# Which engine makes some of layer 3's state sums: 24 additions from VectorE to GpSimd

## The chip, the cores and the metric

The kernel runs on one core of a Trainium2 chip. The core has five engines that work side by side, each through its own queue in order: TensorE (PE in the profile, with its weight loads as PEld), VectorE (DVE), ScalarE (ACT), GpSimd (POOL) and SyncE (SP), which here issues the DMAs. The metric is the device time of one execution in microseconds (us). Before the change it was 6535.2, 6563.37 and 6560.74 us in three runs; the median is 6560.74 us.

## The reference

Four layers are applied to an image `x` of 2 x 128 x 64 x 64: a Mamba block in four directions (layer 0), an attention to a context image (layer 1), a self-attention (layer 2), and a small Mamba block over tokens with a group norm (layer 3). Only layer 3 is touched. Each of the 8192 pixels is a sequence of 8 tokens with 16 channels, so the recurrence has only 8 steps in time, but runs for all pixels at once:

```python
seq = x.transpose(0, 2, 3, 1).reshape(B * H * W, TOKEN_NUM, D_MODEL)   # 8 tokens of 16
dt = jax.nn.softplus(dt @ dt_proj_w.T + dt_proj_b)
dA = jnp.exp(dt[..., None] * A)
dBx = dt[..., None] * Bm[:, :, None, :] * xs[..., None]
def step(h, inp):
    dA_t, dBx_t, C_t = inp
    h = dA_t * h + dBx_t
    return (h, jnp.einsum('nds,ns->nd', h, C_t))
_, ys = jax.lax.scan(step, h0, (dA, dBx, Cm))     # over the 8 tokens
y = (ys + xs * D) * jax.nn.silu(z)
return y @ out_proj_w.T
...
return x + xp        # xp: SiLU of the group norm of the result
```

All is float32. The state `h` has 32 x 16 numbers per pixel.

## The kernel before

Layer 3 cuts the 2 x 4096 pixels into 16 chunks of T = 512 pixels (`ci` = 0 to 15). A chunk has four steps (`k` = 0 to 3), and a step handles two neighbouring tokens (`o` = 0, 1; the first token of step 0 needs no decay, the second of step 3 no sum). For one token the state is a tile of 128 partitions x 4 groups x 512 pixels, and VectorE and GpSimd handle it in two halves of 2 x 512 = 1024 numbers per partition. Each half of each token goes through these operations, which the program abbreviates by a letter:

- `D` (method `db_`, line 1390, VectorE): the term dBx; the B rows, loaded by DMA into the tile D, are multiplied by a PSUM tile `rx` that TensorE made.
- ScalarE (`da_`, line 1397) writes dA = exp(..) into a tile A. One A tile holds both tokens of a step, and there are three of them. It is issued one step ahead.
- `m` (method `mul`, line 1407, GpSimd): A = A * h, where h is the D tile of the token before.
- `v` or `g` (method `add`, line 1412): the sum D = D + A, which is the new state h. `v` means VectorE, `g` means GpSimd. Both operands lie in SBUF.
- `C` (method `hc_`, line 1430, VectorE): A = A * q, where q is a PSUM tile that TensorE (line 1424) spreads from C; it overwrites A, so it comes after the sum has read A. One `C` takes one group of both tokens of a step, and it runs one step later. TensorE then adds the products up into y (line 1440), which releases A.

The two digits behind `m`, `v` and `g` are token and half. The order is written out by hand, with four groups of operations for each step:

```python
PLAN = (
    ("m10 m11 C D", "C D time", "C v10 D", "g11 D C"),
    ("m00 m01 C D v00", "C v01 D m10 m11", "v10 D", "g11 D"),
    ("m00 m01 C D v00", "C v01 m10 m11", "C v10 D", "g11 C"),
    ("m00 m01 C D", "C v00 D g01 m10 m11", "C D", "D C"),
)
```

The program issues these in this order, and each engine takes its own share of them in order. So GpSimd's queue in step 1 and in step 2 is m00 m01 m10 m11 g11, in step 3 m00 m01 g01 m10 m11, in step 0 m10 m11, two more products that `time` stands for (`dt_add`, line 1341, and `dtx_`, line 1344), and g11: 20 operations per chunk. VectorE has 8 sums, 14 `C`, 14 `D` and six small operations in a chunk (lines 1324, 1376, 1445, 1455). The state's dependence runs m00, v00, m10, v10, and then m00 of the next step; the other half runs m01, v01, m11, g11.

GpSimd issues no DMA in layer 3. SyncE's queue loads D and the decays' source dtr for two steps ahead; there are six D tiles.

Of the kernel before, what the change touches and what calls it, by code (L numbers as in the profile page):

```python
# [14 lines left out]
B, C, H, W = 2, 128, 64, 64  # L15
# [41 lines left out]
def conv_seq_kernel(ctx: ExitStack, tc: tile.TileContext, a: dict, out: bass.AP):  # L57
# [40 lines left out]
    with ExitStack() as c0:  # L98
# [397 lines left out]
        with tc.manual_schedule():  # L496
# [114 lines left out]
            for k, c in enumerate(chunks):  # L611
# [3 lines left out]
                def at(u):  # L615
                    return (c, u) if 0 <= u < 16 else ((old, u + 16) if u < 0 else (new, u - 16))
# [3 lines left out]
                A, V, M, G = {}, {}, {}, {}  # L620
# [191 lines left out]
    with ExitStack() as c1:  # L812
# [377 lines left out]
        with tc.manual_schedule():  # L1190
# [22 lines left out]
            for slot in range((len(groups) + 2) * UPG):  # L1213
                u = slot % UPG
                G = at(slot)[0]
# [5 lines left out]
                G, d = at(slot - 1)  # L1221
                if G is not None:
                    G.larger(d)
                G = at(slot - UPG)[0]
# [7 lines left out]
                G, d = at(slot - UPG - 5)  # L1232
                if G is not None and d % 2 == 0:
                    G.prob(d // 2)
                G, d = at(slot - UPG - 6)
                if G is not None and d % 2 == 0:
                    G.expo(d // 2)
                G, d = at(slot - UPG - 8)
                if G is not None:
                    G.value(d)  # L1240
                G, d = at(slot - UPG - 7)
                if G is not None and d % 2 == 0 and d:
                    G.total(d // 2)
                G, d = at(slot - 2 * UPG)
# [13 lines left out]
    with ExitStack() as c3:  # L1258
# [252 lines left out]
        V, G = nc.vector, nc.gpsimd  # L1511
# [9 lines left out]
        def prepare():  # L1521

            nonlocal made
            if made < len(cs):
                c, k, u = cs[made]
                c.pc_(k, u)
                made += 1
# [3 lines left out]

        PLAN = (
            ("m10 m11 C D", "C D time", "C v10 D", "g11 D C"),
            ("m00 m01 C D v00", "C v01 D m10 m11", "v10 D", "g11 D"),
            ("m00 m01 C D v00", "C v01 m10 m11", "C v10 D", "g11 C"),
            ("m00 m01 C D", "C v00 D g01 m10 m11", "C D", "D C"),
        )

# [3 lines left out]
        with tc.manual_schedule():  # L1542
            mm(y, lhsT=ident, rhs=x[:, 0, 0:T], start=True, stop=True)
            c, c1 = chunks[:2]
            c.xs, c.e, c.cb, c.rows, c.ddt = xs0, e0, cb0, rows0, ddt0
            c.spread(0)
            for o in range(2):
                c.load(0, o)
            for o in range(2):
                c.rx_(0, o)  # L1550
            c1.xs = xs1
            c1.dt_(0)
            norms = [Norm(b) for b in range(B)]
            for s in range(-1, len(steps) + 3):
                (pc_, pk), (cc, ck), (nc_, nk) = at(s - 1), at(s), at(s + 1)
                (n2, n2k) = at(s + 2)
                ci, k = divmod(s, 4)
                fut = chunks[ci + 1] if s >= 0 and ci + 1 < len(chunks) else None
                fut2 = chunks[ci + 2] if ci + 2 < len(chunks) else None
                old = chunks[ci - 1] if ci > 0 else None  # L1560
                nrm = norms[0] if ci in (NCH, NCH + 1) else None

                first, extra = {}, {}

                def more(key, *what, at=extra):
                    at.setdefault(key, []).extend(what)

                if fut is not None:  # L1570
                    more((0, 0), fut.b_, at=first)
                    more((0, 1), fut.c_, at=first)
                    more((0, 2), fut.cb_)
                    more((0, 3), fut.put_b, fut.put)
                if old is not None:
                    more((1, 0), lambda: old.yg_(1))
                    more((2, 1), old.xr_, at=first)
                    more((2, 3), old.bn_)
                if cc is not None:
                    more((1, 0), lambda: cc.cbx_(0), at=first)  # L1580
                    more((1, 0), lambda: cc.ecb_(0))
                    more((1, 3), lambda: cc.y0_(0), at=first)
                    more((1, 3), lambda: cc.sz_(0), at=first)
                    more((2, 0), lambda: cc.sz_(1), at=first)
                    more((3, 0), lambda: cc.cbx_(1), at=first)
                    more((3, 0), lambda: cc.yg_(0), lambda: cc.ecb_(1))
                    more((3, 3), lambda: cc.y0_(1), at=first)
                if fut2 is not None and s >= 0:
                    more((1, 1), lambda: fut2.xs_(0), at=first)
                    more((1, 2), lambda: fut2.xs_(1), at=first)  # L1590
                    more((2, 3), lambda: fut2.dt_(0), at=first)
                if fut2 is not None:
                    more((3, 2), lambda: fut2.dt_(1), fut2.e_exp, fut2.e_ln, at=first)
                if 0 <= ci < B:
                    sl = slice(1024 * k, 1024 * k + 1024)
                    more((k, 3), lambda: nc.sync.dma_start(kept[ci][:, sl], x[:, ci, sl]))
                if n2 is not None:
                    more((k, 0), lambda: n2.spread(n2k), lambda: n2.load(n2k, 0))
                    more((k, 1), lambda: n2.load(n2k, 1))
                    more((k, 3), lambda: n2.rx_(n2k, 0), lambda: n2.rx_(n2k, 1))  # L1600
                if ci == NCH:
                    more((3, 2), nrm.first)
                    more((3, 3), nrm.second, nrm.third)
                if ci == NCH + 1:
                    more((0, 1), nrm.fourth)
                    more((1, 2), *[lambda j=j: nrm.silu(j) for j in range(4)])
                    more((1, 2), lambda: nrm.load(0))
                    for j in range(8):
                        at_ = (2 + j // 4, j % 4)
                        if j < 7:  # L1610
                            more(at_, lambda j=j: nrm.load(j + 1))
                        more(at_, lambda j=j: nrm.store(j, (G, V)[j % 2]))

                nd = 0
                for g in range(4):
                    ops = PLAN[k][g].split()
                    if pc_ is None:
                        ops = [o for o in ops if o != "C"]
                    if nc_ is None:
                        ops = [o for o in ops if o != "D"]  # L1620
                    if cc is None:
                        ops = [o for o in ops if o[0] not in "mvg"]
                    if "C" in ops:
                        prepare()


                    if pc_ is not None and pk and g:
                        pc_.y_(pk, g - 1)
                    (older, ok) = at(s - 2)
                    if g == 0 and older is not None and ok:  # L1630
                        older.y_(ok, 3)
                    for f_ in first.get((k, g), []):
                        f_()
                    if g == 0 and nc_ is not None:
                        nc_.da_(nk)
                    for o in ops:
                        if o == "C":
                            c_, k_, u_ = cs[used]
                            c_.hc_(k_, u_)
                            used += 1  # L1640
                        elif o == "D":
                            nc_.db_(nk, nd // 2, nd % 2)
                            nd += 1
                        elif o == "time":
                            if fut is not None:
                                fut.dt_add()
                                fut.dtx_()
                        elif o[0] == "m":
                            cc.mul(ck, int(o[1]), int(o[2]))
                        else:  # L1650
                            cc.add(ck, int(o[1]), int(o[2]), V if o[0] == "v" else G)
                    for f_ in extra.get((k, g), []):
                        f_()
                if s < 0:
                    prepare()
            n1 = norms[1]
            n1.load_all()
            n1.first()
            n1.second()
            n1.third()  # L1660
            n1.fourth()
            for j in range(8):
                if j % 2 == 0:
                    n1.silu(j // 2)
                n1.store(j, V)
# [109 lines left out]
```

## Time and profile before

| What | Value |
|---|---|
| times of three runs, us | 6535.2, 6563.37, 6560.74 |
| the profiled execution's own time (span), us | 6564.3 |
| VectorE busy over the span | 5628.5 us, 86% |
| GpSimd busy over the span | 5420.7 us, 83% |
| layer 3: GpSimd's first and last product (line 1407) start at | 5602.1 us, 6524.6 us |
| sums (line 1412) on VectorE | 128, from 1210 to 3378 ns, median 2461 ns |
| sums (line 1412) on GpSimd | 64, from 2341 to 3358 ns, median 3218 ns |
| products (line 1407) on GpSimd | 224, from 2339 to 3383 ns, median 2361 ns |
| layer 3, 5602 to 6524 us: VectorE, GpSimd, ScalarE, TensorE busy | 856.6, 789.1, 450.1, 808.7 of 922 us |

Layer 3 is the last seventh of the span. All steps are regular but for the first chunk, the end, and chunks 8 and 9, where the group norm and the stores of the first image are woven in. From the start of one chunk on GpSimd to that of the next, the quick ones take 55.64 to 55.77 us (chunks 1, 2, 5, 7, 8, 11, 12 and 13), chunks 4 and 6 take 56.83 us, and chunk 9, with the stores, 71.35 us. A "busy" time of an instruction goes from its start to its end, whatever it does in between.

### The profile page before, as it was taken

Reading aid. Unit: us, or ns where it says so; the run is one execution under the profiler, and the core shown is the slowest. Engines: PE = TensorE matmul, PEld = TensorE weight load, DVE = VectorE, ACT = ScalarE, POOL = GpSimd, SP = SyncE. Lnnn points to the kernel's source line nnn. Section 1 sums busy time; section 2 is a strip of 40 time slices with the busy share of each in tenths; the row PEclk is TensorE's granted clock in tenths of the full one; section 3 lists DMA queues with packets and bytes.
Section 4 is the critical chain, followed back from the end, with each engine's and each line's share of the span. In section 5 each row is a group of like instructions: output and inputs, shape, how many; then the busy total and the mean of one; then the engine's idle time right before and its main releaser. Section 6 shows DMA issues by size and latency. Waiting matters only on the chain. (4 is left out here: it accounts for less than half of the span.)

```text
span 6564.3 us, 66618 instructions
## 1 busy us (share of the span) xinstructions
PE 5817.9 (89%) x20014; PEld 2781.5 (42%) x20014; DVE 5628.5 (86%) x4540; ACT 4487.8 (68%) x7771; POOL 5420.7 (83%) x2543
## 2 busy tenths in 40 slices
PE   8888888888888888888888999999999999898888
PEld 2222222222222222222226888888888788222221
DVE  7999999999999999999997766666666766899997
ACT  7887778877788777887766665555556565555453
POOL 6999999999999999999995666655666566788886
PEclk7888777877788777887779999999999999889897
DMA  6566656566666666556650000000000000877775
GB/s 181 145 156 161 161 142 146 146 150 148 152 155 151 153 152 152 146 146 152 151 137 19 2 4 3 1 1 1 1 1 1 2 6 7 205 173 179 181 180 121
DMA packets 400476, 700.36 MB, mean 107 GB/s; under 512 B 74089, under 2 KB 76658, under 8 KB 399730
## 3 DMA queue, kind: packets, MB, share of 16 engines
q1 hardware_dynamic: 399232, 694.33, 43.3%
q8 instruction: 157, 2.57, 0.2%
q14 instruction: 205, 1.68, 0.1%
q10 hardware_dynamic: 882, 1.78, 0.1%
HBM read 584.53 MB, written 111.28 MB: 106 GB/s over the span
## 5 line engine op out<-in xcount | busy, mean ns | idle before, releaser
L383 POOL TENSOR_TENSOR dbu<-dus,bs 128x1024 f32<-128x1024 f32 x1024 | 2448.1, 2440 | 116.9 <-DVE h L427 98.8
L427 DVE TENSOR_TENSOR_SCAN h<-da,hst,dbu 128x1024 f32<-128x1024 f32 x896 | 2090.9, 2340 | 86.1 <-ACT dbu L411 80.7
L396 ACT ACTIVATE da<-dts,aneg 128x512 f32<-128x512 f32 (+1 forms) x2048 | 1410.1, 689 | 357.1 <-DVE h L427 318.9
L1004 POOL TENSOR_TENSOR sum<-sum,sc 128x1024 f32<-128x1024 f32 x378 | 898.1, 2376 | 504.1 <-ACT sc L999 500.4
L966 ACT COPY sc<-s 128x512 f32<-128x512 f32 x1024 | 596.9, 585 | 767.8 <-PE s L961 639.2
L961 PE MATMUL s<-q,k 128*128 128x256 f32 x4096 | 1053.8, 380 | 9.7 <-ACT lo L919 5.5
L1016 PE MATMUL av<-sc,v 128*128 128x256 f32 x4096 | 1051.2, 380 | 9.1 <-ACT sc L999 9.1
L450 PE MATMUL y<-hc,cst 128*32 128x512 f32 x4096 | 880.4, 753 | 200.2 <-DVE hc L439 186.6
L973 DVE TENSOR_TENSOR mx<-mx,s 128x512 f32<-128x512 f32 x896 | 609.3, 680 | 452.5 <-ACT sc L966 449.2
L439 DVE TENSOR_TENSOR hc<-h,pc 128x1024 f32<-128x1024 f32 x704 | 841.9, 1196 | 9.5 <-PE y L450 7.4
L961 PEld LDWEIGHTS s<-q,k 128*128 128x128 f32 x4096 | 777.0, 191 | 126.9 <-issue 8.8
L1016 PEld LDWEIGHTS av<-sc,v 128*128 128x128 f32 x4096 | 768.0, 190 | 112.9 <-ACT sc L999 14.1
L437 POOL TENSOR_TENSOR hc<-h,cs 128x1024 f32<-128x1024 f32 x320 | 770.0, 2406 | 1.2 <-issue 1.2
L416 PE MATMUL pc<-xd,sel 16*128 16x512 f32 x1024 | 707.0, 780 | 0.2
L1407 POOL TENSOR_TENSOR A<-A,D 128x1024 f32<-128x1024 f32 x224 | 526.9, 2370 | 138.8 <-DVE D L1412 102.1
L996 DVE TENSOR_TENSOR sc<-sc,pm 128x1024 f32<-128x1024 f32 x512 | 620.5, 1212 | 0.9 <-PE pm L992 0.9
L999 ACT ACTIVATE sc<-sc 128x1024 f32<-128x1024 f32 x512 | 541.8, 1058 | 41.2 <-DVE sc L996 41.0
L450 PEld LDWEIGHTS y<-hc,cst 128*32 128x32 f32 x4096 | 125.9, 120 | 858.3 <-DVE hc L439 427.6
L340 PE MATMUL misc<-xd,w_dt 9*128 9x512 f32 x504 | 364.6, 810 | 128.1 <-ACT x L479 68.5
L411 ACT ACTIVATE dbu<-hst,dbu,df 128x1 f32<-128x1 f32 x896 | 337.6, 377 | 65.3 <-POOL dbu L383 42.7
L1424 PE MATMUL q<-xs,room 32*128 32x512 f32 x840 | 291.1, 706 | 63.1 <-DVE A L1430 62.1
L416 PEld LDWEIGHTS pc<-xd,sel 16*128 16x128 f32 x1024 | 181.6, 218 | 350.2 <-issue 296.8
(315 smaller groups left out, 7792.9 us busy)
## 6 DMA issues: line engine op xcount, KB each, us to landing
dts<-ddt SPq DMA_DIRECT2D x512, 256.0 KB, 5.4
dus<-ddu SPq DMA_DIRECT2D x512, 256.0 KB, 5.1
D<-rows SPq DMA_DIRECT2D x448, 256.0 KB, 6.0
bs<-rows SPq DMA_DIRECT2D x1024, 64.0 KB, 4.9
cs<-rows SPq DMA_DIRECT2D x1024, 64.0 KB, 3.2
ddt<-dt SPq DMA_DIRECT2D x128, 256.0 KB, 2.0
ddu<-dtu SPq DMA_DIRECT2D x128, 256.0 KB, 4.0
dtr<-ddt SPq DMA_DIRECT2D x448, 64.0 KB, 2.0
```

What stands on the lines that cost most here:

```text
L383: nc.gpsimd.tensor_mul(t, self.dus[q], _bc(self.bs[g], 1, [P, 2, T]))
L396: act(t[:, i, sl], self.dts[q][:, i, sl], AF.Exp, scale=an[:, g, 2 * q + i : 2 * q + i + 1])
L416: mm(t, lhsT=sel[32:48, 4 * g : 4 * g + 4, :].rearrange("p n d -> p (n d)"), rhs=self.xd[32:48, :], start=True, stop=True)
L427: nc.vector.tensor_tensor_scan(ho, ai, bi, init, ALU.mult, ALU.add)
L437: nc.gpsimd.tensor_mul(t, self.h[u], _bc(self.cs[gq(u)[0]], 1, [P, 2, T]))
L439: nc.vector.tensor_mul(t, self.h[u], _bc(self.pc[u // 2], 1, [P, 2, T]))
L450: mm(self.y[q // 2][r : r + 32, :], lhsT=sum4, rhs=self.hc[u][:, i, :], start=False, stop=(u % 8 >= 6), skip_group_check=True)
L961: mm(p[:, o, :], lhsT=j.k[m // 8][:, m % 8 * P : m % 8 * P + P], rhs=self.q, start=True, stop=True)
L973: nc.vector.tensor_max(self.mx, self.s[0][:, 0:2, :] if u == 1 else self.mx, self.p[u])
L996: nc.vector.tensor_sub(s, s, _bc(self.pm[:, :], 1, [P, 4, NQ]))
L1004: self.adds.tensor_add(self.sum, self.s[0] if w == 1 else self.sum, self.s[w])
L1016: mm(self.av, lhsT=self.job.v[m // 8][:, m % 8, :], rhs=self.s[u // 2][:, m % 4, :], start=(m == 0), stop=(m == 31))
```

## The change

The third of VectorE's three sums in step 2, v10, becomes g10 in all 16 chunks. The one in step 1 becomes h10, a new letter, which means VectorE in chunks of odd `ci` and GpSimd in those of even `ci`. The place in the plan stays. So 16 + 8 = 24 sums change engine: 104 are left on VectorE, 88 are on GpSimd.

```diff
         PLAN = (
             ("m10 m11 C D", "C D time", "C v10 D", "g11 D C"),
-            ("m00 m01 C D v00", "C v01 D m10 m11", "v10 D", "g11 D"),
-            ("m00 m01 C D v00", "C v01 m10 m11", "C v10 D", "g11 C"),
+            ("m00 m01 C D v00", "C v01 D m10 m11", "h10 D", "g11 D"),
+            ("m00 m01 C D v00", "C v01 m10 m11", "C g10 D", "g11 C"),
             ("m00 m01 C D", "C v00 D g01 m10 m11", "C D", "D C"),
         )
...
-                        ops = [o for o in ops if o[0] not in "mvg"]
+                        ops = [o for o in ops if o[0] not in "mvgh"]
...
-                            cc.add(ck, int(o[1]), int(o[2]), V if o[0] == "v" else G)
+                            cc.add(ck, int(o[1]), int(o[2]), V if o[0] == "v" or o[0] == "h" and ci % 2 else G)
```

GpSimd's queue in such a step is then m00 m01 m10 m11 followed by the moved sum and g11. The order on TensorE, ScalarE and SyncE is the same as before.

## The prediction

> **What bounds the kernel now.** The busy times by stretch come first, for two stretches inside layer 3 (columns: us, then busy time and instructions of TensorE, its weight loads, VectorE, ScalarE and GpSimd, the granted TensorE clock, DMA share, GB/s).
>
> ```profile
> 5800.00:5900.00 100.00, 91.19 (x290) 23.85 (x290) 96.49 (x75) 49.93 (x58) 87.73 (x36) 0.90 0.77 176
> 5900.00:6000.00 100.00, 89.13 (x274) 23.33 (x270) 96.36 (x74) 48.49 (x56) 86.48 (x36) 0.90 0.77 173
> ```
>
> VectorE looks like the bound, 96% busy, with GpSimd at 87%. The groups by line say what that busy time is (the number after the busy time is the mean of one in ns):
>
> ```profile
> L1412 DVE TENSOR_TENSOR D<-D,A 128x1024 f32<-128x1024 f32 x128 | 294.7, 2302 | 4.7 <-POOL A L1407 4.0
> L1430 DVE TENSOR_TENSOR A<-A,q 128x1024 f32<-128x1024 f32 x224 | 268.5, 1208 | 15.7 <-PE q L1424 15.7
> L1390 DVE TENSOR_TENSOR D<-D,rx 128x1024 f32<-128x1024 f32 x224 | 268.2, 1209 | 36.3 <-PE q L1424 21.3 <-DMA D<-rows 12.7 <-DMA dtr<-ddt 1.5
> L1412 POOL TENSOR_TENSOR D<-D,A 128x1024 f32<-128x1024 f32 x64 | 185.2, 2894 | 3.7
> ```
>
> Three VectorE operations of one size: the two that read PSUM take 1.21 us, the sum, whose operands both lie in SBUF, 2.30. The shortest sum took 1.21 too. GpSimd's sums take 2.89 on average, 2.34 at the shortest. The timeline of one step shows why (start, duration, engine, line). These are v00, C, v01, C, v10 of step 2 in chunk 4 on VectorE, and on GpSimd m00 m01, m10, m11, g11, and step 3's m00 m01:
>
> ```profile
> 5865.98 3.37 DVE L1412 TENSOR_TENSOR D<-D,A 128x1024 f32<-128x1024 f32 x1
> 5869.28 1.21 DVE L1430 TENSOR_TENSOR A<-A,q 128x1024 f32<-128x1024 f32 x1
> 5870.41 2.46 DVE L1412 TENSOR_TENSOR D<-D,A 128x1024 f32<-128x1024 f32 x1
> 5872.79 1.21 DVE L1430 TENSOR_TENSOR A<-A,q 128x1024 f32<-128x1024 f32 x1
> 5873.92 2.47 DVE L1412 TENSOR_TENSOR D<-D,A 128x1024 f32<-128x1024 f32 x1
> ...
> 5863.59 4.68 POOL L1407 TENSOR_TENSOR A<-A,D 128x1024 f32<-128x1024 f32 x2
> 5869.43 2.35 POOL L1407 TENSOR_TENSOR A<-A,D 128x1024 f32<-128x1024 f32 x1 [1.16 <-DVE D L1412]
> 5872.94 2.36 POOL L1407 TENSOR_TENSOR A<-A,D 128x1024 f32<-128x1024 f32 x1 [1.16 <-DVE D L1412]
> 5875.39 3.23 POOL L1412 TENSOR_TENSOR D<-D,A 128x1024 f32<-128x1024 f32 x1
> 5878.57 4.70 POOL L1407 TENSOR_TENSOR A<-A,D 128x1024 f32<-128x1024 f32 x2
> ```
>
> m01 ends at 5863.59 + 4.68 = 5868.27, and v00, which began 2.29 earlier, ends 1.08 after it. m10 ends at 5871.78, v01 1.09 later. m11 ends at 5875.30, v10 1.09 later. Then g11, begun at 5875.39, ends at 5878.62, which is 2.23 after v10. So a VectorE sum and a GpSimd operation never run together: whoever comes second waits, and then takes its own 1.1 or 2.3 us. The PSUM operations run freely beside GpSimd. VectorE's 96% is filled up with waiting.
>
> What is never free is this common **turn**. A quick chunk on GpSimd (chunk 5, from its first product at 5891.52 to the next chunk's at 5947.17) takes 55.65 us. Its 20 GpSimd operations at 2.34 (half of 4.68) are 46.8 us, and 8 VectorE sums at 1.1 are 8.8: together 55.6. Nothing is left. VectorE's own work in a chunk is only 28 x 1.13 (the distance of two in a row) + 8 x 1.1 + 6 x 0.61 = 44 us. GpSimd's idle time says the same: nearly all of it is the turn of a VectorE sum, 1.16 at a time.
>
> ```profile
> POOL A L1407 <- DVE D L1412: 102.1, 69, 6.3
> ```
>
> **The change, part by part.** *The moved sum itself.* Today the stretch from the end of m11 to the end of g11 is 5878.62 - 5875.30 = 3.32: v10's turn and then g11. Read in the timelines of all chunks, the 24 steps concerned have 3.29 to 3.31, but for one with 7.65 (chunk 9, with stores in between). Afterwards GpSimd makes two operations back to back there, 4.69 (the 4.68 and 4.70 above). That is 1.38 more, 24 times: **33.1 us**. A GpSimd sum that nobody holds up is in the trace (2341 ns), so this price has no unknown in it; the 2.47 us that VectorE loses each time buys nothing by itself.
>
> *What follows in step 3.* Today v00 of step 3 starts at 5883.94, just after g01 has begun (5883.36), waits for it, and m10 idles 1.16 behind it, to 5886.86. Afterwards m11 still ends at 5875.30, the moved sum at 5877.65, g11 at 5879.99, m00 at 5882.34, m01 at 5884.68. VectorE, without v10, has done D, C and the statistics by 5876.8, and the next C (today 5879.18) reads what the moved sum leaves free, so it now waits for GpSimd, to 5877.7. Behind it queue D, two small operations, a C and v00: 5883.94 - 5879.18 = 4.76 later, at 5882.5. That is after m00 and inside m01, so v00 gets its turn at 5884.68 and ends at 5885.77; g01, held up, ends 3.31 after m01, at 5887.99, and m10 follows at 5888.05. Instead of 1.38 GpSimd is 1.19 late. In 16 chunks this saves 16 x 0.19 = **3.0 us**. The new wait is 0.9 us on VectorE and costs nothing while v00 is ready before 5884.68, a margin of 2.2 us. In step 2 after a moved step-1 sum, only C and D stand between that wait and v00, and v00 lands in m01 as today.
>
> *What VectorE gains.* From there VectorE is 1.0 us earlier and GpSimd 1.2 later, so VectorE has 2.2 us more in hand before step 1. That can fill gaps in which both sat still for the sums of steps 0 and 1: 1.32 and 2.32 in chunk 3, 1.06 in chunk 4, 1.09 in chunk 6, 2.19 in chunk 10, 8.0 us in all. In chunk 4 it lies behind TensorE at a granted clock of 0.77 and 0.74 (5849 to 5853 and 5853 to 5856). Bounds: 0 and 8.0. I take a quarter, 2, since a slow stretch of the clock need not fall on the same steps again.
>
> *Queues.* No DMA is moved or added. D tiles come free with GpSimd's products, so loads start later together with it; the loads' cover is two steps, some 30 us, against 5 or 6 us for a load.
>
> The sum against the profiled execution: 6564.3 + 33.1 - 3.0 - 2 = 6592.4. That execution lies 3.6 us above the median of the runs, less than the runs' spread of 28 us; I leave it there: **6592 us**, 31 above the median.
>
> A rule that bears on this: the Trainium skill (Perfetto Trace Analysis, Optimizing Scalar/DVE Operations) says that a saturated VectorE may hand work to GpSimd, and warns that the two share an SBUF read port, so it may not help. By its first half the sum would be the first rival's below, by its warning about nothing; the rows above say more than either, a loss.
>
> **The rivals.** *VectorE is the bound after all.* For it: 96% busy. Then each moved sum gives back its whole 2.47 us: 24 x 2.47 = 59.3, or 6564.3 - 59.3 = **6505 us**. It decides if VectorE's own work per chunk exceeds some 55 us, so that GpSimd's 1.16 us gaps are lateness of VectorE. Against it: 44 us of own work, and sums that end 1.08 or 1.09 us after a GpSimd operation again and again. Chance 0.08.
>
> *GpSimd's idle time takes the sums.* For it: 12 to 13 us in 100 are idle, 6.8 per chunk, and the move adds 2.3 or 4.7 of work. Then GpSimd would not end later: **6564 us**, a little less with the gaps filled. Against it: the idle time lies in the VectorE sums' turns, which stay for 104 of 128. With all gaps and more recovered, 6566 to 6580. Chance 0.10.
>
> *The new wait bites.* 24 times a C now stands behind GpSimd's sum, and TensorE's q and y, then ScalarE's A, behind that C. VectorE has waited for TensorE up to 4.2 us at once (13 waits of 21.3 us together), above the margin of 2.2. If v00 comes late by the difference, 1 to 2 us, in all 16 chunks, it is 16 to 32 us more: **6608 to 6624 us**. Against it: C runs a whole step behind its products, and VectorE has more spare time than before. Chance 0.09.
>
> That the sums are not moved at all is excluded by the diff: the letter alone chooses the engine.
>
> **How the numbers follow.** The forecast, port turns as the bound, has 0.73. Its own range is 6564.3 + 33.1 - 3.0 - 8.0 = 6586 to 6564.3 + 33.1 = 6597, and with the spread of the runs about 6580 to 6606. About 0.5% of 6560.74, 33 us, is what a measurement of this kernel can tell from no change, so 6593.5 is where "slower" begins; the forecast lies on this line. I put 0.42 of it above (a slow clock gives other gaps, and the first chunk and the end have waits that can grow) and 0.31 below. Slower: 0.42 + 0.09 = 0.51; same: 0.31 + 0.10 = 0.41; faster: 0.08. The range 6566 to 6616 leaves out the first rival, the lower end of the second and the upper half of the third.
>
> **What would show it.** In the new profile the moved sums should take 2.34 us right behind m11, with no 3.2 us g11 after them; VectorE's sums should still end 1.1 after a GpSimd operation; a chunk with odd number should take about 55.65 + 1.2 = 56.8 us and one with even number about 55.65 + 1.2 + 1.4 = 58.2; GpSimd's busy share should rise and VectorE's fall. The step-3 part is right if v00 now ends 1.1 after m01 and g01 takes 3.3. The forecast is wrong if chunks stay at 55.65, or if gaps of more than 1.2 us before GpSimd's products become frequent.

## The result, and the profile after

The changed kernel takes 6585.76 us (median of five runs, 6582.05 to 6592.93) against 6560.74 (five runs, 6535.2 to 6563.37). The ratio is 1.0036 with a 95% interval of 1.0021 to 1.0052: slower by 25 us, clear of the spread of the runs, and smaller than the 0.5% that the prediction named as what can be told. The profiled execution has a span of 6580.2 us, 15.9 above the one before.

The busy times of the same two stretches of layer 3 as before the change come first, with the same columns. VectorE has fallen from 96% to 87 and 91%; the granted TensorE clock was 0.85 and 0.90.

```profile
5800.00:5900.00 100.00, 87.86 (x262) 22.26 (x264) 87.08 (x69) 49.61 (x55) 84.65 (x37) 0.85 0.71 166
5900.00:6000.00 100.00, 89.66 (x290) 22.01 (x282) 90.72 (x73) 51.36 (x58) 91.19 (x39) 0.90 0.80 182
```

So the engine that looked saturated got 24 operations less, and the time rose. The groups by line show that GpSimd's sums became shorter on average (2579 ns after 2894), because neither the 24 moved ones nor the g11 behind them are held up, and that VectorE's did not (2347 after 2302). VectorE's sums now wait 30.0 us for GpSimd's products (the last number of the first row), where the prediction's row had 4.0:

```profile
L1412 DVE TENSOR_TENSOR D<-D,A 128x1024 f32<-128x1024 f32 x104 | 244.1, 2347 | 30.4 <-POOL A L1407 30.0
L1412 POOL TENSOR_TENSOR D<-D,A 128x1024 f32<-128x1024 f32 x88 | 225.8, 2579 | 1.9
```

The timeline of the same step as before, step 2 of chunk 4 (VectorE's v00 and v01 and the first C of step 3; then GpSimd's m00 m01, m10, m11, and the moved sum with g11):

```profile
5885.04 3.37 DVE L1412 TENSOR_TENSOR D<-D,A 128x1024 f32<-128x1024 f32 x1 [1.81 <-POOL A L1407]
...
5889.47 2.46 DVE L1412 TENSOR_TENSOR D<-D,A 128x1024 f32<-128x1024 f32 x1
...
5896.72 1.22 DVE L1430 TENSOR_TENSOR A<-A,q 128x1024 f32<-128x1024 f32 x1 [0.79 <-POOL D L1412]
...
5882.64 4.70 POOL L1407 TENSOR_TENSOR A<-A,D 128x1024 f32<-128x1024 f32 x2
5888.49 2.36 POOL L1407 TENSOR_TENSOR A<-A,D 128x1024 f32<-128x1024 f32 x1 [1.16 <-DVE D L1412]
5892.01 2.36 POOL L1407 TENSOR_TENSOR A<-A,D 128x1024 f32<-128x1024 f32 x1 [1.16 <-DVE D L1412]
5894.32 4.67 POOL L1412 TENSOR_TENSOR D<-D,A 128x1024 f32<-128x1024 f32 x2
```

v01 still ends (5891.93) 1.08 us after m10 (5888.49 + 2.36 = 5890.85): the two engines still take turns. From the end of m11 (5894.37) to the end of g11 (5898.99) it is 4.62 us; before the change it was 3.32. The first C of step 3 now waits 0.79 us for GpSimd. In the waits of the whole layer that is a new row, beside the one that the prediction showed, which has fallen from 102.1 to 84.1:

```profile
POOL A L1407 <- DVE D L1412: 84.1, 63, 4.7
...
DVE A L1430 <- POOL D L1412: 22.8, 22, 1.4
```

**Where the 15.9 us between the two profiled executions are.** I laid the timelines of the two kernels side by side, chunk by chunk. From the first product of chunk 0 to the end of the last one of chunk 15, GpSimd takes 939.9 us after 924.9, that is 15.0 more: 23 of the 24 stretches from m11 to g11 went from 3.30 to between 4.61 and 4.66, and the one with stores in between stayed at 7.6. At 1.32 each, 23 moves are 30.4 us. Step 3 is 0.3 shorter in nine chunks (12.6 after 12.93), which gives back 2.7. The gaps in which neither GpSimd nor a VectorE sum ran (those over 0.3 us) fell from 29.6 to 17.2, which gives back 12.4. Together 30.4 - 2.7 - 12.4 = 15.3, where 15.0 were measured.

Two large differences outside of the loop nearly cancel, and I put neither down to the moved sums. Layer 3 began 12.9 us later after the change, with the same program in front of it; in the experiments below, whose layers 0 to 2 are untouched too, the first copy of B (line 1313) starts anywhere from 5610.5 to 5626.9 us (5608.9 before, 5622.9 after). And what follows the last product of GpSimd, a chain of TensorE and VectorE, took 37 us before the change and 25 after it. These two stretches are shown here, before and then after (columns as above):

```profile
6527.00:6564.00 37.00, 23.38 (x50) 5.12 (x50) 12.72 (x22) 8.05 (x8) 0.01 (x1) 0.59 0.15 57
```

```profile
6555.00:6580.00 25.00, 10.97 (x41) 3.19 (x40) 11.50 (x21) 8.05 (x8) 0.00 (x0) 0.77 0.23 84
```

The granted clock was 0.59 in the one and 0.77 in the other: it stood at half speed from 6513 to 6547 us in the execution before the change. In the 14 traces of this case, experiments included, this tail took 21.9 to 25.4 us where its mean clock was 0.74 to 0.78, and 32.2 to 38.5 us where it was 0.59 to 0.61. So of the 15.9 us of the pair, 15.0 is the loop, and I count the 12.9 and the -11.9 as chance; the 25 us of the medians are the better measure of the change, and lie between the 15.0 of this pair's loop and the 30.4 of the moves alone.

### The profile page after: what moved, and what is told of

The parts are those of the page before. It is cut to its first block, busy times and chain, and to the rows that moved or that the text cites. A ratio compares the mean times of both kernels' runs of the same rounds, so it can differ in the third digit from the quotient of the medians.

```text
span 6580.2 us, 66627 instructions
## 1 busy us (share of the span) xinstructions
PE 5794.5 (88%) x20014; PEld 2775.5 (42%) x20014; DVE 5588.5 (85%) x4516; ACT 4489.6 (68%) x7771; POOL 5484.8 (83%) x2567
## 5 line engine op out<-in xcount | busy, mean ns | idle before, releaser
L1407 POOL TENSOR_TENSOR A<-A,D 128x1024 f32<-128x1024 f32 x224 | 527.5, 2374 | 116.4 <-DVE D L1412 84.1
```

## The experiments

All were timed in five rounds beside the kernel before, whose median was 6561.7 us beside experiments 1 to 4, 6566.3 beside 5 and the first three kernels of 7, 6567.1 beside 6 and the last two of 7, and 6562.8 beside 8. Ratios are to that kernel.

**1. The 24 sums left out.** Against the changed kernel, in the loop over the plan (`p` stands for step 2's sum):

```diff
-                        else:
+                        elif o[0] == "p" or o[0] == "h" and ci % 2 == 0:
+                            pass
+                        else:
                             cc.add(ck, int(o[1]), int(o[2]), V if o[0] == "v" or o[0] == "h" and ci % 2 else G)
```

> The 24 sums that the change moves are left out on both engines (the state of half 0 lacks a term, so the output differs from the reference's); all else is as before. Theory (a VectorE sum and a GpSimd operation take turns, and the turn is the bound of layer 3): each sum left out gives back the 0.96 us that g11 was held up (3.30 to 2.34), 24 x 0.96 = 23 us, so about 6538 us, ratio 0.9965. Rival A (VectorE's time is the bound): 24 x 2.47 = 59 us less, 6501 us. Rival B (GpSimd's queue alone is the bound, its own operations and the waits for v00 and v01, and VectorE's v10 doesn't touch it): nothing changes, 6561 us.

Measured: 6534.16 us, ratio 0.9950 (0.9936 to 0.9965), 28 us less. The theory said 23, VectorE's time 59, GpSimd's queue alone 0. Both rivals fall.

**2. The 24 sums on VectorE, with one operand in PSUM.** In place of `pass` above:

```diff
+                            if nc_ is not None:
+                                d_ = cc.D[ck, 1][:, 0:2, :]
+                                V.tensor_add(d_, d_, _bc(nc_.rx[nk, nd // 2], 1, [P, 2, T]))
```

> The 24 sums stay on VectorE in the same place, with the same size and output, but the second operand is the PSUM tile rx in place of A in SBUF (the state of half 0 gets a wrong term, so the output differs from the reference's). Theory: with only one operand in SBUF the sum needs no turn; it should take 1.21 us like C and D, g11 2.34, and the time should be that of the kernel without the 24 sums, about 6538 us, to within 5 us, since VectorE has time to spare. Rival A (VectorE's time): 24 x 1.21 = 29 us slower than without them, 24 x 1.26 = 30 us faster than before, 6531 us. Rival C (any two operations side by side slow each other, whatever they read): the sum still takes some 2.4 us, g11 3.3, and the time is that of before, 6561 us.

Measured: 6536.91 us, ratio 0.9958 (0.9944 to 0.9972): the time of experiment 1 to within 3 us, as if the 24 sums weren't there. Rival C, which said 6561, falls. Rival A's 6531 is too near to be told from this time, but its sums should have cost 29 us against experiment 1. This is the timeline of step 2 of a chunk in experiment 2: v01, C and the sum that reads PSUM (line 1653) on VectorE, then m10, m11 and g11 on GpSimd.

```profile
5863.56 2.46 DVE L1412 TENSOR_TENSOR D<-D,A 128x1024 f32<-128x1024 f32 x1
5865.94 1.21 DVE L1430 TENSOR_TENSOR A<-A,q 128x1024 f32<-128x1024 f32 x1
5867.07 1.21 DVE L1653 TENSOR_TENSOR D<-D,rx 128x1024 f32<-128x1024 f32 x1
...
5862.59 2.35 POOL L1407 TENSOR_TENSOR A<-A,D 128x1024 f32<-128x1024 f32 x1 [1.16 <-DVE D L1412]
5866.10 2.36 POOL L1407 TENSOR_TENSOR A<-A,D 128x1024 f32<-128x1024 f32 x1 [1.16 <-DVE D L1412]
5868.53 2.37 POOL L1412 TENSOR_TENSOR D<-D,A 128x1024 f32<-128x1024 f32 x1
```

v01, with two operands in SBUF, waits for m10 and takes 2.46. The sum of the same size in the third row runs inside m11 (5866.10 to 5868.46) in 1.21, and neither m11 (2.36) nor g11 (2.37) notices. All 24 took 1208 ns on average. The sum that reads PSUM doesn't need m10 either, but that isn't the difference: in the prediction's rows v10 began 2.1 us after m10 had ended (5873.92 and 5871.78). So what costs is the pair of SBUF operands on VectorE beside a GpSimd operation, and not VectorE's time. The change puts a GpSimd operation in place of such a turn, which makes the stretch 4.62 us long where it was 3.30; that is the loss. The Trainium skill (SBUF — State Buffer, SBUF: two separate sides) names the mechanism: a VectorE operation with two SBUF inputs and a GpSimd operation that reads SBUF lock a shared port pair for a whole instruction, and the loser blocks. Both rows agree with it, 2.46 us with and 1.21 without a second SBUF operand.

**3. Twice the dose: v10 to GpSimd in steps 0, 1 and 2 of all chunks, 48 sums.**

```diff
-            ("m10 m11 C D", "C D time", "C v10 D", "g11 D C"),
-            ("m00 m01 C D v00", "C v01 D m10 m11", "v10 D", "g11 D"),
-            ("m00 m01 C D v00", "C v01 m10 m11", "C v10 D", "g11 C"),
+            ("m10 m11 C D", "C D time", "C g10 D", "g11 D C"),
+            ("m00 m01 C D v00", "C v01 D m10 m11", "g10 D", "g11 D"),
+            ("m00 m01 C D v00", "C v01 m10 m11", "C g10 D", "g11 C"),
```

> All three v10 of a chunk (steps 0, 1 and 2) go to GpSimd in all chunks: 48 sums, twice the change. Theory: each costs about 1.32 us of turns, as in the trace of the changed kernel, 63 us, less some 8 us of filled gaps: about 6610 us (6600 to 6625), ratio 1.0075. Rival D (the loss of the change is no price per sum but a one-off, such as the 13 us by which layer 3 began later, and TensorE's clock): about 6586 us as with 24.

Measured: 6615.23 us, ratio 1.0077 (1.0062 to 1.0091), 54 us more, in the forecast range; 25 with 24 sums. The loss goes with the number, 1.0 to 1.1 us a sum. The rival of a one-off falls.

**4. The opposite move: GpSimd's four sums of a chunk to VectorE, 64 sums.** Here g11 becomes v11 in steps 0, 1 and 2, and g01 becomes v01 in step 3.

> The opposite move: GpSimd's four sums of a chunk (g11 of steps 0, 1, 2 and g01 of step 3), 64 in all, go to VectorE, and the 128 there stay. Theory: a GpSimd sum takes 2.34 us of turns, a VectorE sum 1.0 to 1.1, so 64 x 1.25 = 80 us less if VectorE keeps up (own work 44 + 4 x 1.1 = 48 us in a chunk, turns 16 x 2.34 + 12 x 1.1 = 51): 6481 us; with new gaps, since VectorE then has little to spare, up to 6520. Rival A (VectorE's time is the bound): 64 x 1.1 to 2.4 us more, 6630 to 6715 us.

Measured: 6677.80 us, ratio 1.0176 (1.0160 to 1.0192). The theory was wrong here, in the sign and by at least 158 us. It lies in the range of rival A, VectorE's time, 6630 to 6715. These are the busy times in a stretch and GpSimd's largest wait in layer 3:

```profile
5800.00:5900.00 100.00, 89.40 (x246) 22.25 (x242) 89.30 (x72) 47.42 (x52) 59.79 (x26) 0.82 0.67 158
```

```profile
POOL A L1407 <- DVE D L1412: 305.3, 142, 7.6
```

GpSimd is busy 60% and waits 305 us for VectorE's sums, up to 7.6 at once; before the change it was 102, mostly a turn at a time. So the turns are the bound in one direction only. I read it as VectorE's queue standing nearly as close behind: the 44 us of own work that the prediction gave it per chunk leave out what it stands still for, in its turns and for TensorE. TensorE's clock is lower in this stretch too, 0.82 after 0.90 before the change, and what part that has was not tried.

**5. The smallest opposite move: g11 of step 2 to VectorE, 16 sums.** The plan's row 2 ends in `"C v10 D", "v11 C"`.

> One sum per chunk goes the other way: g11 of step 2 becomes VectorE's, 16 in all, the rest as before the change. Theory 1 (only the turn bounds): 16 x 1.25 = 20 us less, 6542 us. Theory 2 (the kernel before stands where two bounds meet: the turns, 55.65 us in a chunk, and VectorE's queue with the time it stands still for its turns, 28 x 1.13 + 6 x 0.61 + 8 x 2.2 = 53 us, and some 2 us more of waits for TensorE): one more sum costs VectorE its 2.2 us, so 57.3 us in a chunk, 16 x 1.7 = 27 us more, 6588 us.

Measured: 6598.34 us, ratio 1.0055 (1.0043 to 1.0068), 32 us more. Theory 2 forecast 27 more. One sum more per chunk on VectorE loses, as 1.5 fewer did in the change. GpSimd's steps show where. Apart from the first chunk and chunk 9, step 2 takes 13.0 us after 15.0 before the change, steps 0 and 1 take no longer than they did, and step 3 takes 15.8 to 18.3 after 12.93. In step 3 m10 waits for v00, 1.16 us in most chunks before the change and 2.5 to 5.3 now (chunk 9 apart), and it starts 0.08 us after v00 in all 16 chunks. These are GpSimd's waits for VectorE in 13 chunks (5640 to 6450 us), before the change and then here:

```profile
POOL A L1407 <- DVE D L1412: 82.1, 61, 3.6
```

```profile
POOL A L1407 <- DVE D L1412: 124.6, 77, 5.3
```

So the second bound is VectorE's queue between v11 and v00 of step 3. In chunk 4 VectorE works through it without a pause; in chunk 5 it also stands 2.5 us for TensorE there.

**6. The same sum reading PSUM.** The one sum of experiment 5 gets rx as operand, as in experiment 2.

> As the run with g11 of step 2 on VectorE (16 sums, 6598 us), but this one sum reads the PSUM tile rx in place of A, so that it needs no turn (the state of half 1 gets a wrong term in step 2, so the output differs from the reference's). It asks how much of VectorE's price for a sum is the sum and how much the standing still. Theory 2: VectorE pays 1.13 us in place of 2.2, the turns lose 2.34: VectorE 53 + 1.1 + 2 of waits = 56.2 us in a chunk, 0.5 above before, about 6575 us (6560 to 6582). Rival (the place in the queue matters, not the turn): 6598 us again.

Measured: 6605.61 us, ratio 1.0058 (1.0043 to 1.0072). That is experiment 5 again, as the rival forecast, and not the 6575 of my second theory: that VectorE's price for the sum is its standing still was wrong, or not all. The sum itself did need no turn (1208 ns each). The waits of the kernel in 13 chunks (5640 to 6450 us), first of GpSimd, then of VectorE:

```profile
POOL A L1407 <- DVE D L1412: 146.0, 78, 5.1
```

```profile
DVE A L1430 <- PE q L1424: 20.5, 8, 3.2
DVE D L1390 <- PE q L1424: 19.3, 7, 3.3
```

In the same stretch GpSimd waited 82.1 us for VectorE before the change, and 124.6 in experiment 5. What the turns gave back, GpSimd waited longer for VectorE's sums, above all v00 of step 3, which stands behind two C, a D and two small operations: in the chunk shown below it waited 5.11 us for it. All of VectorE's waits for TensorE were 74 us, against 26 before and 19 in experiment 5. From its first product on GpSimd to that of the next chunk, a chunk took 57.5 to 58.2 us six times and 61.4 to 61.6 seven times (the first and chunk 9 apart). Before each of the slow ones TensorE went to half clock for 20 us, from step 3 of the chunk before into step 0 (from 5717, 5837, 5960 and 6079 us, for instance); this is one of these stretches in that kernel's busy times, and behind it a stretch at full clock:

```profile
5837.00:5857.00 20.00, 20.00 (x39) 4.10 (x40) 13.15 (x13) 7.01 (x9) 12.93 (x6) 0.50 0.89 191
...
5866.00:5883.00 17.00, 14.71 (x44) 4.38 (x42) 16.89 (x16) 10.08 (x12) 13.01 (x6) 1.00 0.77 175
```

The half clock is not the whole of it. Step 3 takes 16.8 to 16.9 us after 12.93 in all chunks but the first and chunk 9, with a mean clock of 0.59 or of 0.80. What goes with the clock is step 0, 12.6 to 13.2 us at 1.00 and 15.1 at 0.77 or 0.78, and step 1 behind it, 15.1 and 16.6. Whether the half clock makes these two slow, or their rhythm brings the half clock, was not tried. The sum also keeps rx longer (TensorE's rx products waited 6.3 us for it), so the experiment isn't clean.

**7. GpSimd relieved of `time`, with three plans.** TensorE adds dt and e in PSUM, ScalarE copies the result, and VectorE multiplies by xs. Not shown are the plan, which loses the word `time`, and the place in step 0 where the new operations are issued:

```diff
-            def dt_add(self):
-                nc.gpsimd.tensor_add(self.dt, self.dt, self.e)
-            def dtx_(self):
-                nc.gpsimd.tensor_mul(self.e, self.dt, self.xs)
+            def dts_(self, i):
+                p = self.pt = misc()
+                mm(p, lhsT=ident, rhs=self.dt[:, i, :], start=True, stop=False)
+                mm(p, lhsT=ident, rhs=self.e[:, i, :], start=False, stop=True)
+                nc.scalar.copy(self.dt[:, i, :], p)
+            def dtx_(self, i):
+                nc.vector.tensor_mul(self.e[:, i, :], self.xs[:, i, :], self.pt)
```

With the plan before:

> No sum is moved against the kernel before, but the two GpSimd operations that stand for the word time in the plan go: TensorE adds dt and e up in PSUM, ScalarE copies the result out, and VectorE multiplies the PSUM tile by xs, two halves of 512. GpSimd is left with 18 operations in a chunk. Theory 2: turns 55.65 - 2 x 2.34 = 51.0 us, VectorE 53 + 2 x 0.6 + 2 of waits = 56: VectorE now bounds, so little changes, 6555 to 6575 us. Theory 1: 16 x 4.7 = 75 us less, 6487 us.

With step 2's move:

> As the last, and the change's move in step 2 (g10 in all 16 chunks). Theory 2: VectorE 56 - 2.2 = 54, turns 51.0 + 1.3 = 52.3, so about 54 us in a chunk, 16 x 1.7 = 27 us less than before, 6535 us: the move that costs 1.3 us in the change is a gain once the turns are not the bound. Theory 1: turns alone, 16 x 3.4 = 54 us less than before and 21 us more than the kernel without the move.

With the whole change:

> As the last but one, and the whole change (24 sums on GpSimd). Theory 2: VectorE 56 - 1.5 x 2.2 = 52.7, turns 51.0 + 1.5 x 1.3 = 53: the two meet again, about 53.3 us in a chunk, 16 x 2.3 = 37 us less than before, 6525 us. Theory 1: 43 us less than before and 32 us more than the kernel without the moves.

Measured: 6679.91, 6663.86 and 6700.20 us, ratios 1.0177 (1.0158 to 1.0196), 1.0154 (1.0140 to 1.0168) and 1.0206 (1.0192 to 1.0220). All lose, and all lie over 100 us above what either theory said. A new wait shows. In the first of them:

```profile
POOL A L1410 <- DVE D L1415: 238.4, 66, 14.6
...
DVE e L1347 <- ACT dt L1344: 87.9, 24, 5.0
```

VectorE stands 3.7 us on average before each of its products, for a copy by ScalarE that lies behind other work in that queue, and GpSimd, without `time` to fill the stretch, waits up to 14.6 us for v10 behind it. Step 2's move seems to gain 16 us on this ground, the direction that theory 2 gave it, but the intervals overlap; the whole change lies 20 us above the kernel without moves.

The second attempt put the products one group later and v10 of step 0 one group earlier.

> The run with TensorE's addition of dt and e and with g10 in step 2 again (6664 us), with its products by xs one group later, so that VectorE doesn't wait for ScalarE's copies (24 waits of 88 us were seen in 12 chunks), and v10 of step 0 one group earlier, since GpSimd waited up to 14.6 us for it. Theory 2: without these waits VectorE's 54 us or the turns' 52.3 bound: 6535 to 6560 us. If another wait takes their place, above 6600.

> The same with the whole change, 24 sums on GpSimd (6700 us before the two waits were treated). Theory 2: VectorE 53, turns 53: 6525 to 6555 us. If another wait takes their place, above 6600.

Measured: 6597.40 us, ratio 1.0048 (1.0035 to 1.0062), and 6622.91, ratio 1.0085 (1.0071 to 1.0099). The first lies between its two forecasts, the second where another wait was forecast. The second attempt took back most of the loss, 66 and 77 us, and VectorE's wait for the copies fell from some 88 us to 33 and 38. But no version beats the kernel before, and what remains is open. The eight h10 of the second cost 26 us more than without them.

**8. v00 of step 3 earlier, the kernel before otherwise.**

```diff
-            ("m00 m01 C D", "C v00 D g01 m10 m11", "C D", "D C"),
+            ("m00 m01 C D v00", "C D g01 m10 m11", "C D", "D C"),
```

> The kernel before with one edit: v00 of step 3 stands one group earlier, behind m00 m01 C D as in steps 1 and 2, in front of two small operations and a C. It takes by itself what the prediction booked as a side effect in step 3. Theory: v00 then takes its turn behind m01 and not behind g01, m10 has no wait left, and step 3 on GpSimd takes 12.63 us (as in nine chunks of the changed kernel) in place of 12.93, 16 x 0.3 = 5 us less, 6560 us; VectorE's C of step 3 comes 2 us later, which has slack. Rival (the C held back delays TensorE and the next step): 6570 us or more.

Measured: 6601.16 us, ratio 1.0054 (1.0041 to 1.0068). Step 3 did become shorter, 12.56 to 12.64 us after 12.93, but for chunk 9 with the stores. But step 0 went from 12.65 to between 14.3 and 16.6 in eleven chunks, and step 1 from 15.1 to 16.6 in most of these. This is GpSimd's new wait in step 0 (13 chunks), for ScalarE's logarithm:

```profile
POOL dt L1341 <- ACT e L1338: 21.9, 11, 2.6
```

ScalarE's work there starts from a product of TensorE's, which stood at half clock there (0.50 from 5850 to 5860 and 0.51 from 5730 to 5744); VectorE's waits for TensorE were 55 us against 26. The local gain was real, some 0.35 us in each of 15 chunks, 5 us, and 43 were lost behind it. The time is in the rival's range, and the rows show a delay by TensorE; whether it comes from the C held back, as the rival said, or from the clock, is open.

## Why the prediction was right

*What bounds the kernel.* Right for the direction of the change, and shown: 48 and 24 sums on GpSimd cost 54 and 25 us, and 24 sums left out give 28 (experiments 3 and 1), and the turn is what does it (experiment 2). Too strong in "VectorE's own work in a chunk is only" 44 us: its queue has no room for even one sum more in step 2 (experiment 5), and that VectorE is the bound holds for sums that come to it. Too strong also in "nearly all" of GpSimd's idle time: the wait for VectorE's sums was 102.1 of 133 us (922 less 789.1).

*The moved sum.* 1.38 was expected, from 3.31 (4.69 less the 3.32 of the one step worked out would be 1.37) to two operations back to back; 1.32 was measured, since two sums in a row took 4.61 to 4.66 and not 4.69. With one move of no cost (chunk 9) the term is 30.4 us in place of 33.1.

*Step 3.* 0.19 in all 16 chunks was expected; it came as 0.3, in nine chunks (5 to 8 and 11 to 15). The term is 2.7 in place of 3.0. In six of the others (0 to 4 and 10), the chunk of the worked example among them, v00 still came 0.4 to 1.2 us after g01 had begun. The new wait of C was 0.8 us in five of these, about as worked out (0.9), and 1.4 in chunk 0; but the D behind it then stood another 2.4 to 3.1 us, for TensorE in chunks 1 to 4 and for a DMA in 0 and 10, which the prediction had not counted. In chunk 3 the granted clock was 0.50 and 0.57 there (5835 to 5839 and 5839 to 5843 us). These are its C, D and v00:

```profile
5838.42 1.22 DVE L1430 TENSOR_TENSOR A<-A,q 128x1024 f32<-128x1024 f32 x1 [0.78 <-POOL D L1412]
5842.69 1.22 DVE L1390 TENSOR_TENSOR D<-D,rx 128x1024 f32<-128x1024 f32 x1 [3.05 <-PE q L1424]
...
5846.48 2.38 DVE L1412 TENSOR_TENSOR D<-D,A 128x1024 f32<-128x1024 f32 x1
```

*The filled gaps.* This is the mis-sized term: 2 us of 8.0 were taken, and 12.4 were filled in the profiled pair. 5.0 of the 8.0 went; most of the rest lay near the end, where four gaps of 7.2 together, one in chunk 14 and three in chunk 15, vanished. The medians leave only 3 us for it (30.4 - 2.7 - 25), so part of the 12.4 seems to be chance, and that the 2 comes near these 3 owes something to luck.

*The rivals.* VectorE's time: out by experiment 1. Free idle time of GpSimd: out by experiment 3. The new wait of C: it is there, 22.8 us in all, and came too late for the margin of 2.2 us in six chunks, because of the further wait behind it. It cost little all the same: v00 fell back to the place it had before the change, so what was lost is the saving of 0.3 us in these chunks, not 1 to 2 us in all 16.

*The test rows.* Odd chunks took 56.7 to 57.0 and even ones 57.95 to 58.42, but for chunks 0, 3, 9 and 10 (56.8 and 58.2 expected). GpSimd's busy share in layer 3 rose from 85.6 to 88.7% and VectorE's fell from 92.9 to 87.0%. The median, 6585.76, is 6 us under the forecast. The terms by themselves add up to 28 us, against 25 measured; the rest of the 6 is the 3.6 us by which the span of the profiled execution lay above the median of the times (a span is some 2 us shorter than the time of its execution, 6580.2 and 6582.05 after the change). The result is on the near side of the 6593.5 us where "slower" was to begin, so the side that was given 0.41 came, not the one with 0.51; the interval shows all the same that a loss of 0.36% can be told from none here.

## What to carry to other kernels

Before moving an elementwise operation between VectorE and GpSimd, see from the timeline whether the two ever run at once: if each of VectorE's operations with both operands in SBUF ends one own duration after a GpSimd operation, they take turns, the price of a move is the difference of the two durations on that common account (here 2.34 against 1.0), and a busy share of 96%, which counts the standing still, does not say what VectorE gives back when work is taken from it. An operand in PSUM takes an operation off that account (experiment 2), which helps only where the queue behind it has room (experiment 6). And where two accounts are both full, as here, single operations lost in both directions; look for what removes work, and expect a local gain to be spent in the next wait.

## What the runs showed that I had not expected

TensorE's granted clock, which I had treated as noise, went along with the outcome of several experiments; whether it is their cause was not tried. It drops to 0.5 in stretches of 3.4 to 41 us (the longest in experiment 3); with one such stretch the end of the kernel took 37 us in place of 25, and in experiments 6 and 8 stretches of 7 to 20 us stood on the same steps in chunk after chunk, with VectorE's waits for TensorE two to three times those before the change. An edit that touches no TensorE work (experiment 8) moved the time by half a per cent in such company. The Trainium skill (TensorE: Matmul & The Clock Gate, What's actually happening) has the half rate end after about 3.4 us of sustained activity; the row of experiment 6 doesn't fit that, with TensorE shown busy for all of 20.0 us at 0.50.
